# Eight batches of block 4's keys and values made around the last batch's routing, in place of two behind it

## The chip, the cores and the metric

The kernel runs on one core of a Trainium2 chip. The metric is the time of one execution on the device, in microseconds (us). A core has five engines with instruction queues of their own: TensorE (PE; its weight loads are shown as PEld), VectorE (DVE), ScalarE (ACT), GpSimd (POOL) and SyncE (SP, which only issues DMAs here). Each works its queue off in order and waits at semaphores.

## The reference

A decoder of two layers on 16 sequences ("batches" below) of 256 rows by 256 columns, in float32, with residual additions. Cut to what matters here, its six blocks are:

```python
x = x + self_attention_16_heads(layernorm(x))                       # block 0
x = x + cross_attention_16_heads(layernorm(x), ctx, mask)           # block 1
t = rmsnorm(layernorm(x)) * norm_weight                             # block 2: experts
g, e = top_k(t @ gate_w.T, 2)                                       # routing
x = x + layernorm(x) + sum(softmax(g)[k] * mlp(expert e[k], t))
x = x + linear_attention(layernorm(x))                              # block 3
x = x + cross_attention(layernorm(x), ctx @ Wk.T, ctx @ Wv.T)       # block 4
x = x + gated_expert_attention(layernorm(x))                        # block 5
```

The keys and values of block 4, `ctx @ Wk.T` and `ctx @ Wv.T`, depend on nothing but the inputs. They can be made at any time before block 4.

## The kernel before

The whole of x stays on the chip (`xs[b]`, 128 partitions by 2 by 256 for each batch). The work is staged:

- Stage 0 and 1 (pool `s01`, blocks 0 and 1): a software pipeline over `duos`, the 2 x 16 x 4 pairs of head pairs. `step(n)` (L638) issues the projections of duo n, the scores of n-1, the transposes of n-2 and the weighted sums of n-3. Behind the pipeline, a generator `route(b)` (L515) for each batch does the routing of block 2. It is resumed once per step; what lies between two of its `yield`s goes into one step. For the last batch, 15, step 131 (`len(duos) + 3`) starts it (norm of the rows, store of them to `hd`), step 133 makes the transposes `ps_hT` (L543), step 134 the logits `lgp` (L547) and from them on VectorE the two largest and the gates, step 136 the counts `pp` (L586), `cps` and the four scatters into `perms` (L608), step 137 `pb` (L620) and the last addition to x (L623). Batch 14 is four steps ahead: its `pp` and `cps` are in step 132, its `pb` in step 133.
- Stage 2 (pool `s2`, block 2): set-up from the counts, `plan()` (L818, first matmuls `ps_tok`, L821), then 71 expert tiles.
- Stage 3 (pool `s3`, block 3): `SETS`, four for each batch; `step3(s)` (L1119) issues the scores of set s (`scores3`, L1035), the weighted sums of s-2 and the finish of s-3, and at given sets of a batch the gather, sums, statistics, norm (`normed3`, L983, whose `h` is written at L988), transposes (`rows3`, L997) and projections of later batches.
- Stages 4 and 5: blocks 4 and 5.

The order of TensorE's instructions is the order in which they are written (`tc.manual_schedule`), in stage 3 that of VectorE too. The other queues are ordered by a planner, which takes the instruction that it expects to be ready.

`context4(b, ...)` (L289) is a generator that makes the keys and the values of block 4 for batch b. Its three pieces are: the load of the transposed ctx rows `c` (`ctx_rows`, L78, 256 KB on SP); the keys, 8 matmul records `ps_k`, a copy to `k4` on ScalarE (L297) and the store to `kd` from ScalarE's queue (L298); the values, `ps_v`, `v4` (L304) and `vd` (L305), likewise. `fill(gens, n, ahead)` (L308) resumes the first unfinished generator n times, and each time that one ends, it starts the load of the one that stands `ahead` places behind.

Two batches (`EARLY`) are made at the end of stage 1: their generators and weights `w4` are set up at step 127, and `fill(early, 2 * EARLY)` (L715) runs all four halves behind the last step, so behind the last batch's `pb`. Their tiles are slots of pool `s01`: `c` has two, which block 1's ctx rows use too, `k4` takes those of `qk`, and `v4` those of `v`, six of which two hold the weights. The other 14 batches are made in stage 3 (`late`): eight halves by `fill(late, 8, 2)` (L1165) ahead of the steps, three in each of the steps -3, -2 and -1, and one in each of the steps 0 to 10 (L1168).

Behind the last early half the pool `s01` is closed. The next instructions are memsets of `ve` on GpSimd (L728), loads of `ph` from `perms` on SP (L756) and a chain of small operations from `ti` (L761) to `pick` (L810), which `plan` needs; their tiles lie where those of `s01` lay.

Of the kernel before, what the change touches and what calls it, by code (L numbers as in the profile page):

```python
# [10 lines left out]
F32 = mybir.dt.float32  # L11
# [6 lines left out]
P = 128  # L18
D = 256
S = 256  # L20
NEG = -3.0e38
EARLY = 2


@with_exitstack
def decoder(ctx: ExitStack, tc: tile.TileContext, a: dict, out: bass.AP):
# [48 lines left out]

    dram = ctx.enter_context(tc.tile_pool(name="dram", bufs=1, space=bass.MemoryType.DRAM))

    def ctx_rows(b, pool, bufs=2):  # L78

        ct = pool.tile([P, 2, S], F32, tag="c", name="c", bufs=bufs)  # L80
        nc.sync.dma_start(
            out=ct, in_=a["ctxT"][:, b * S : (b + 1) * S].rearrange("(c p) s -> p c s", p=P)
        )
        return ct
# [111 lines left out]
    def two_k(ps, lhsT, rhs):  # L196

        for c in range(2):
            nc.tensor.matmul(ps, lhsT=lhsT(c), rhs=rhs(c), start=(c == 0), stop=(c == 1))  # L199
# [88 lines left out]

    def context4(b, pool, mm, wk, wv, kt, vt, cpool=None):  # L289

        ct = ctx_rows(b, cpool or pool, 3 if cpool else 2)
        yield
        ps = mm([P, 2, S], "ps_k4")
        for m in range(2):
            two_k(ps[:, m, :], lambda c: wk[:, c, m * P : (m + 1) * P], lambda c: ct[:, c, :])
        k = pool.tile([P, 2, S], F32, tag=kt[0], name="k4", bufs=kt[1])
        nc.scalar.copy(k, ps)  # L297
        nc.scalar.dma_start(out=kds[b], in_=k)  # L298
        yield
        ps = mm([P, 2, D], "ps_v4")  # L300
        for t in range(2):
            two_k(ps[:, t, :], lambda c: ct[:, c, t * P : (t + 1) * P], lambda c: wv[:, c, :])
        v = pool.tile([P, 2, D], F32, tag=vt[0], name="v4", bufs=vt[1])
        nc.scalar.copy(v, ps)  # L304
        nc.scalar.dma_start(out=vds[b], in_=v)  # L305
        yield

    def fill(gens, n, ahead=1):  # L308

        for _ in range(n):  # L310
            while gens and next(gens[0], 0) == 0:
                gens.pop(0)
                if len(gens) > ahead:
                    next(gens[ahead])
# [32 lines left out]
    with ExitStack() as st:  # L347
        pool = st.enter_context(tc.tile_pool(name="s01", bufs=2))
# [35 lines left out]
        def rows_T(l, b):  # L384
            ps = transposed(hs[l, b], psum, "mm", bufs=4)
            hTs[l, b] = hp.tile([P, 2, S], F32, tag="hT", name="hT")
            nc.scalar.copy(hTs[l, b], ps)
# [247 lines left out]
        duos = [(l, b, d) for l in range(2) for b in range(NB) for d in range(4)]  # L635
        routing = []

        def step(n):  # L638
            at = [duos[n - k] if 0 <= n - k < len(duos) else None for k in range(4)]
            new, sc, tr, av = at  # L640

            if n >= 4 and n - 4 < len(duos) and duos[n - 4][2] == 3:
                output(duos[n - 4][0], duos[n - 4][1], 1)
            if sc:
                for i in range(2):
                    scores(sc[0], sc[1], 2 * sc[2] + i)
            if av:
                for i in range(2):
                    weighted(av[0], av[1], 2 * av[2] + i)
            others = []  # L650
            if av and av[2] == 3:
                others.append(lambda: output(av[0], av[1], 0))
            if new:
                l, b, d = new
                nxt = duos[n + 4] if n + 4 < len(duos) else None
                if d < 3:
                    others.append(lambda: values(l, b, d + 1))
                if nxt and d == 1:
                    prepare(nxt[0], nxt[1])
                if nxt and d == 2:  # L660
                    others.append(lambda: rows_T(nxt[0], nxt[1]))
                if nxt and d == 3:
                    others.append(lambda: values(nxt[0], nxt[1], 0))
            turns = [[] for _ in range(4)]
            if new:
                for i in range(4):
                    turns[i].append(lambda i=i: project(l, b, 2 * d + i // 2, i % 2))

            rest = [x for t in turns for x in t] + others
            trs = []  # L670
            if tr:
                trs = [lambda i=i: heads_T(tr[0], tr[1], 2 * tr[2] + i // 2, i % 2) for i in range(4)]
            for i, x in enumerate(rest):
                x()
                if i >= 1 and trs:
                    trs.pop(0)()
            for x in trs:
                x()
            for g in list(routing):
                if next(g, 0) == 0:  # L680
                    routing.remove(g)
            if n >= 4 and n - 4 < len(duos) and duos[n - 4][0] == 1 and duos[n - 4][2] == 3:
                routing.append(route(duos[n - 4][1]))
                next(routing[-1])

        with tc.manual_schedule(engines={mybir.EngineType.PE}):
            prepare(0, 0)
            rows_T(0, 0)
            values(0, 0, 0)
            n = 0  # L690
            early = []
            while n < len(duos) + 4 or routing:
                if n == 2:
                    wts[1] = load_attention("x0")
                    for p in perms:
                        nc.sync.dma_start(out=p.rearrange("(p f) o -> p (f o)", p=P), in_=zero)
                if n == 4 * NB + 4:
                    load_moe()
                if n == len(duos) - 1:
                    w4 = []  # L700
                    for name, cols in (("x1_wqk", slice(D, 2 * D)), ("x1_wv", slice(0, D))):
                        w = pool.tile([P, 2, D], F32, tag="v", name="w4", bufs=6)
                        nc.sync.dma_start(
                            out=w, in_=a[name][:, cols].rearrange("(c p) e -> p c e", p=P)
                        )
                        w4.append(w)
                    early = [
                        context4(b, pool, mm_tile, *w4, ("qk", 2), ("v", 6))
                        for b in range(EARLY)
                    ]  # L710
                    next(early[0])
                    next(early[1])
                step(n)
                n += 1
            fill(early, 2 * EARLY)  # L715

# [13 lines left out]
    with ExitStack() as st:  # L732
        pool = st.enter_context(tc.tile_pool(name="s2", bufs=2))
# [19 lines left out]
        for i in range(4):  # L753
            for hf in range(2):
                n = P * P
# [196 lines left out]
    with ExitStack() as st:  # L952
        pool = st.enter_context(tc.tile_pool(name="s3", bufs=2))
# [155 lines left out]
        def added3(b):  # L1109
# [3 lines left out]

        late = [
            context4(b, pool, mm3, wxqk[:, :, D : 2 * D], wxv, ("k4", 1), ("v4", 1), vep)
            for b in range(EARLY, NB)
        ]
# [107 lines left out]
    with ExitStack() as st:  # L1225
        pool = st.enter_context(tc.tile_pool(name="s4", bufs=2))
# [170 lines left out]
    with ExitStack() as st:  # L1397
        pool = st.enter_context(tc.tile_pool(name="s5", bufs=2))
# [161 lines left out]
```

## Time and profile before

| What | Value |
|---|---|
| median of 3 runs | 3849.63 us (3846.42 to 3852.25) |
| the profiled execution's own time | 3849.59 us |
| its span, first to last instruction | 3847.9 us |
| granted TensorE clock over the span | 0.99 |
| TensorE, VectorE, ScalarE, GpSimd busy | 97%, 59%, 42%, 27% |
| DMA | 171.44 MB, mean 45 GB/s |
| HBM read, written | 139.57 MB, 27.69 MB |

A row of a timeline gives the start in us from the span's first instruction, the duration, the engine, the line of the kernel, the operation, the tile written and the tiles read, the shapes and the number of instructions merged; in brackets stands how long the engine had been idle before and what ended the wait. A row of a table of stretches gives the stretch, its length, the busy time of PE, PEld, DVE, ACT and POOL with the number of instructions, the granted TensorE clock (1.00 is full), the share of time in which the 16 DMA engines were busy, and GB/s. TensorE's busy time holds matmuls whose ends are modelled, so a busy TensorE isn't always at its peak.

Stage 1 ends at about 1677 us, the early batches run until 1686, `plan` begins at 1697, the last expert tile ends at 1976, and stage 3 lasts from there to about 2338.

### The profile page before, as it was taken

The page shows a single profiled execution, that of the slowest core. Times are in us where ns is not written, and L with a number is a line of the kernel's source. Part 1 is how long each engine was busy: PE and PEld are TensorE (multiplying, and loading weights), DVE is VectorE, ACT ScalarE, POOL GpSimd, SP SyncE. Part 2 cuts the span into 40 slices and gives each one's busy share as a digit, 9 for nine tenths or more (in the row PEclk, how much of TensorE's full clock was granted, in tenths as well). Part 3 has the DMA queues.
Part 4 walks back from the last instruction along what each step waited for, and adds up shares of the span by engine and source line. Part 5 has one row for each costly group of instructions (what it writes and reads, how often), then busy time and mean ns, then how long its engine had stood idle before and what let it go on. Part 6 is the DMA issues. An engine that isn't in the chain of part 4 may idle for free.

```text
span 3847.9 us, 64735 instructions
## 1 busy us (share of the span) xinstructions
PE 3716.0 (97%) x23638; PEld 2715.6 (71%) x23638; DVE 2276.2 (59%) x6213; ACT 1618.1 (42%) x4871; POOL 1041.1 (27%) x1467
## 2 busy tenths in 40 slices
PE   8999999999999999979999889999999999999999
PEld 6777776777777777759987666665666666666666
DVE  6666667645555555532226786776655555555554
ACT  4555554555555555524445555665221222122111
POOL 3332332233343343332225553222000000000100
PEclk9999999999999999979999999999999999999999
DMA  5000000010000000032234000001222222222222
GB/s 196 1 1 1 1 1 1 1 58 15 12 17 18 9 18 17 18 91 72 71 120 151 28 19 25 29 29 24 69 60 59 62 68 61 61 59 66 62 62 50
DMA packets 88268, 171.44 MB, mean 45 GB/s; under 512 B 12448, under 2 KB 60584, under 8 KB 79760
## 3 DMA queue, kind: packets, MB, share of 16 engines
q1 hardware_dynamic: 74384, 141.16, 13.5%
q0 software_dynamic: 8528, 17.74, 1.7%
q10 hardware_dynamic: 5040, 8.40, 0.6%
q8 instruction: 189, 3.10, 0.3%
q14 instruction: 127, 1.04, 0.1%
HBM read 139.57 MB, written 27.69 MB: 43 GB/s over the span
## 4 chain that ended last, share of the span: by engine, by line
PE 87%; DVE 11%; issue 1%; ACT 1%; POOL 0%; DMA 0%; DVEq 0%; POOLq 0%; ACTq 0%
PE ps_qk L199 14%; PE po L1468 11%; PE ps_ve L199 11%; PE ps_v L199 7%; PE tr L268 6%; PE po L505 6%; PE sc L237 4%; PE ps_h L199 3%; PE po L892 3%; PE av L274 3%; PE sc L433 2%; PE av L490 2%; PE sc L1315 2%; PE sc L1289 2%; PE zt L1328 1%; DVE sc L443 1%
## 5 line engine op out<-in xcount | busy, mean ns | idle before, releaser
L258 POOL TENSOR_TENSOR pr<-pr,sm 128x256 f32<-128x256 f32 (+1 forms) x384 | 310.2, 829 | 1449.0 <-DVE sm L256 1337.5
L252 ACT ACTIVATE pr<-sc,nmx 128x128 f32<-128x128 f32 (+1 forms) x768 | 315.3, 417 | 350.8 <-DVE nmx L250 313.6
L1468 PE MATMUL po<-w_oe,ut 128*128 128x256 f32 x2048 | 452.4, 379 | 0.0
L199 PE MATMUL ps_ve<-w_ve,hT 128*128 128x512 f32 x1024 | 450.9, 593 | 0.0
L1468 PEld LDWEIGHTS po<-w_oe,ut 128*128 128x128 f32 x2048 | 388.8, 190 | 52.9 <-issue 0.2
L269 ACT COPY pT<-tr 128x512 f32<-128x512 f32 (+1 forms) x256 | 136.1, 532 | 649.8 <-PE tr L268 649.8
L268 PEld LDWEIGHTS tr<-ident,pr 128*128 128x128 f32 x2176 | 270.8, 141 | 167.9 <-issue 117.5
L268 PE MATMUL tr<-ident,pr 128*128 128x128 f32 x2176 | 346.7, 275 | 13.6 <-ACT zT L499 10.3
L199 PEld LDWEIGHTS ps_ve<-w_ve,hT 128*128 128x128 f32 x1024 | 191.3, 190 | 215.3 <-issue 207.1
L448 ACT ACTIVATE pr<-sc,nmx 128x256 f32<-128x256 f32 x512 | 237.1, 472 | 251.1 <-DVE nmx L443 174.2
L454 POOL TENSOR_TENSOR pr<-pr,sm 128x512 f32<-128x512 f32 x256 | 264.4, 1055 | 282.6 <-DVE sm L452 141.9
L1440 DVE TENSOR_TENSOR tv<-ps_ve,gm 128x512 f32<-128x512 f32 x256 | 176.4, 689 | 204.9 <-PE ps_ve L199 198.2
L443 DVE CUSTOM_DVE_ANT_0 sc<-sc,mk 128x256 f32<-128x256 f32 x512 | 211.0, 443 | 112.0 <-PE sc L433 59.4
L250 DVE TENSOR_REDUCE nmx<-sc 128x2 f32<-128x256 f32 (+1 forms) x384 | 208.1, 556 | 110.1 <-ACT pr L252 105.4
L199 PE MATMUL ps_qk<-hT,w_a 128*128 128x256 f32 x1024 | 259.8, 387 | 0.0
L269 DVE COPY pT<-tr 128x384 f32<-128x384 f32 (+1 forms) x384 | 223.1, 594 | 19.1 <-PE tr L268 13.1
L199 PEld LDWEIGHTS ps_qk<-hT,w_a 128*128 128x128 f32 x1024 | 180.6, 191 | 29.4 <-issue 11.8
L199 PE MATMUL ps_qk<-hT,w 128*128 128x256 f32 x768 | 183.3, 382 | 0.7 <-DVE zn L939 0.7
L1295 DVE TENSOR_REDUCE nm<-sc 128x4 f32<-128x1024 f32 x128 | 150.7, 1220 | 33.6 <-PE sc L1289 33.6
L237 PE MATMUL sc<-qk 64*128 64x128 f32 (+1 forms) x1536 | 160.9, 341 | 4.7 <-ACT pr L252 2.1
L868 DVE COPY wt<-m_w 128x1024 f32 x71 | 49.3, 694 | 188.0 <-PE ps_h L199 186.2
L1459 DVE TENSOR_TENSOR ut<-gr,av 128x1024 f32<-128x1024 f32 x128 | 155.0, 1212 | 5.1 <-PE av L279 5.1
(277 smaller groups left out, 7020.8 us busy)
## 6 DMA issues: line engine op xcount, KB each, us to landing
gr<-gd SPq DMA_DIRECT2D x128, 512.0 KB
yd<-y SPq DMA_DIRECT2D x71, 128.0 KB
c<-in_ctxT SPq DMA_DIRECT2D x32, 256.0 KB
m_w<-in_m_w SPq DMA_DIRECT2D x16, 512.0 KB
x<-in_x SPq DMA_DIRECT2D x16, 256.0 KB
mk<-in_mask SPq DMA_DIRECT2D x16, 256.0 KB
hd<-h SPq DMA_DIRECT2D x16, 256.0 KB
kd<-k ACTq DMA_DIRECT2D x16, 256.0 KB
```

Source lines behind the costliest of these rows:

```text
L199: nc.tensor.matmul(ps, lhsT=lhsT(c), rhs=rhs(c), start=(c == 0), stop=(c == 1))
L237: nc.tensor.matmul(sc[:, j, at : at + ks], lhsT=qk[rows, 0, qs], rhs=qk[rows, 1, 0:ks], start=True, stop=True,)
L250: nc.vector.tensor_reduce(nmx[:, qt, :], sc[:, :, sl], AX.X, ALU.max, negate=True)
L252: nc.scalar.activation(pr[:, j, sl], sc[:, j, sl], AF.Exp, bias=nmx[:, qt, j : j + 1], accum_out=sm[:, qt, j : j + 1],)
L258: nc.gpsimd.tensor_tensor(pr[:, :, sl], pr[:, :, sl], sm[:, qt, :].unsqueeze(2).to_broadcast([P, 2, n]), ALU.mult,)
L268: nc.tensor.transpose(tr[:, at : at + P], src, ident)
L269: copy(pT, tr[:, 0 : P * len(blocks)])
L443: nc.vector.tensor_tensor_reduce(out=sc[:, j, t, :], in0=sc[:, j, t, :], in1=mk[:, t, :], scale=-1.0, scalar=3.4e38, op0=ALU.add, op1=ALU. ...
L448: nc.scalar.activation(pr[:, j, t, :], sc[:, j, t, :], AF.Exp, bias=nmx[:, j, t : t + 1], scale=-1.0, accum_out=sm[:, j, t : t + 1],)
L454: nc.gpsimd.tensor_tensor(pr[:, j], pr[:, j], sm[:, j, :].unsqueeze(2).to_broadcast([P, 2, S]), ALU.mult)
L505: nc.tensor.matmul(po, lhsT=zTs[l, b, c][:, t * P : (t + 1) * P], rhs=wts[l][3][:, c, :], start=(c == 0), stop=(c == 7),)
L1468: nc.tensor.matmul(po[:, t, :], lhsT=ut[:, e, t * P : (t + 1) * P], rhs=woe[hp][:, e, :], start=(hp == 0 and e == 0), stop=(hp == 3 and e ...
```

## The change

`EARLY` becomes 8. Three loads are started at step 127. Behind step 132 (batch 14's `pp` and `cps`; batch 15 is being normalised) four halves are run, behind step 135 (batch 15's logits are being sorted out) two, and behind the last step all that are left, which are ten. The ctx rows of the early batches take the slots of `c` and of `mk`, block 1's mask tile, in turn. Stage 3 has eight batches left, sixteen halves, in the same calls of `fill`.

```diff
-EARLY = 2
+EARLY = 8
...
-    def ctx_rows(b, pool, bufs=2):
+    def ctx_rows(b, pool, bufs=2, tag="c"):
-        ct = pool.tile([P, 2, S], F32, tag="c", name="c", bufs=bufs)
+        ct = pool.tile([P, 2, S], F32, tag=tag, name="c", bufs=bufs)
...
     def context4(b, pool, mm, wk, wv, kt, vt, cpool=None):
-        ct = ctx_rows(b, cpool or pool, 3 if cpool else 2)
+        if cpool:
+            ct = ctx_rows(b, cpool, 3)
+        else:
+            ct = ctx_rows(b, pool, 2, ("c", "mk")[b % 2])
...
-                    next(early[0])
-                    next(early[1])
+                    for g in early[:3]:
+                        next(g)
                 step(n)
+                if n == len(duos) + 4:
+                    fill(early, 4, 2)
+                if n == len(duos) + 7:
+                    fill(early, 2, 2)
                 n += 1
-            fill(early, 2 * EARLY)
+            fill(early, 2 * EARLY, 2)
```

## The prediction

> **What bounds the kernel now.** I read the page's busy shares first, then the table of stretches around the last batch's routing, the timeline of TensorE there, the chain that ended last across it, and the table of stretches by batch of stage 3.
>
> ```profile
> span 3847.9 us, 64735 instructions
> PE 3716.0 (97%) x23638; PEld 2715.6 (71%) x23638; DVE 2276.2 (59%) x6213; ACT 1618.1 (42%) x4871; POOL 1041.1 (27%) x1467
> ```
>
> TensorE is busy for 97% of the span, so work moved helps only where TensorE now waits, and only if nothing else ends last where it came from. The stretches (us; busy time of PE, PEld, DVE, ACT, POOL; granted clock; DMA share and GB/s) of the routing's end:
>
> ```profile
> 1655.00:1665.50 10.50, 1.68 (x10) 0.93 (x9) 5.65 (x32) 0.36 (x1) 5.12 (x5) 0.61 0.70 225
> 1665.50:1676.70 11.20, 6.75 (x22) 4.64 (x22) 4.32 (x28) 1.15 (x3) 1.05 (x2) 0.50 0.39 72
> 1676.70:1686.10 9.40, 9.40 (x33) 7.59 (x32) 0.69 (x1) 1.76 (x3) 2.81 (x3) 0.76 0.21 63
> 1686.10:1697.40 11.30, 0.02 (x1) 0.00 (x0) 5.45 (x29) 0.59 (x1) 3.71 (x24) 0.74 0.80 224
> ```
>
> TensorE is nearly idle in the first and the last of them, and its clock is down to a half in the second. The same in TensorE's timeline (start, duration, in brackets the idle time before):
>
> ```profile
> 1655.15 0.38 PE L616 MATMUL cps<-ident,cb 128*8 128x128 f32 x2
> 1656.04 1.12 PE L622 MATMUL pb<-b,cT 8*128 8x256 f32 x4 [0.51 <-ACT cT L618]
> 1665.47 1.30 PE L191 MATMUL ps_hT<-ident,h 128*128 128x128 f32 x4 [8.31 <-DVE h L535]
> 1672.16 0.61 PE L588 MATMUL pp<-both,tri 128*128 128x16 f32 x2 [2.78 <-DVE both L570]
> 1676.71 3.78 PE L199 MATMUL ps_k<-c,w 128*128 128x256 f32 x8
> 1684.23 1.89 PE L199 MATMUL ps_v<-w,c 128*128 128x256 f32 x8
> 1697.47 0.89 PE L821 MATMUL ps_tok<-pick,ph 128*128 128x71 f32 x3 [11.35 <-DVE pick L810]
> ```
>
> So the three gaps: 8.31 us (rows of batch 15 being normalised), 2.78 us (its two largest logits), 11.35 us (between the early batches and `plan`). The third is no free room. What follows the last early matmul, in time order:
>
> ```profile
> 1686.15 0.59 ACT L304 COPY v<-ps_v 128x512 f32<-128x512 f32 x1 [1.14 <-PE ps_v L199]
> 1686.77 0.33 ACTq L305 DMA_DIRECT2D vd<-v  x1
> 1689.23 1.85 POOL L728 MEMSET ve<- 128x1024 f32 x2 [9.11 <-DMA vd<-v]
> 1691.33 0.20 DVE L763 CAST tf<-ti 128x71 f32<-128x71 int32 x1 [13.82 <-POOL ti L761]
> ```
>
> GpSimd, idle for 9.11 us, starts the next stage's set-up only when the last early batch's store has landed, and `pick`, which `plan` needs, follows from that. The 11.35 us are a tail behind the last early batch, wherever that ends. And the four-set batches 0 to 5 of stage 3, from one batch's first score matmul to the next's (same columns):
>
> ```profile
> 2013.25:2032.26 19.01, 19.01 (x159) 14.91 (x158) 11.59 (x31) 12.01 (x24) 9.45 (x10) 1.00 0.53 170
> 2032.26:2053.41 21.15, 21.15 (x202) 16.45 (x201) 13.01 (x40) 12.85 (x27) 8.96 (x8) 1.00 1.07 379
> 2053.41:2075.11 21.70, 21.32 (x201) 16.36 (x200) 14.57 (x48) 12.67 (x26) 10.29 (x18) 1.00 0.42 145
> 2075.11:2093.95 18.84, 17.05 (x177) 12.06 (x176) 13.76 (x45) 9.88 (x21) 10.66 (x15) 1.00 0.10 29
> 2093.95:2113.85 19.90, 16.97 (x176) 12.16 (x176) 15.80 (x50) 10.78 (x24) 11.62 (x21) 1.00 0.10 28
> 2113.85:2135.19 21.34, 17.75 (x177) 13.01 (x177) 15.90 (x50) 10.70 (x24) 11.62 (x21) 0.92 0.09 25
> ```
>
> The first three carry 4, 4 and 3 half batches (a K or a V, 8 matmul records, 1.73 us apart where they run back to back at full clock, as from 1978.51 to 1980.24) and have TensorE full; the next three carry none and are hardly shorter: there TensorE waits 2.2 us a batch for `h` (L988) of VectorE. Nine such batches, from the score matmuls at 2093.95 to those at 2278.72, take 184.77 / 9 = 20.5 us each. What the fills cost in stage 3 is thus far less than their 1.73 us.
>
> **The change, part by part.** Six batches (12 halves) leave stage 3; four halves go into the first gap, two into the second, ten, instead of four, behind the routing.
>
> *First gap.* 4 x 1.73 = 6.9 us start at 1655.53, behind batch 14's `cps`. `pb` of batch 14 (1.12 us) is queued behind them and ends at about 1663.6, still before `h` is there (1665.47): no cost. If that cover were gone, each half is 1.73 us. On the way: per batch one 256 KB load on SP (0.41 us of issue, loaded ahead: c of batch 1 was issued at 1631.70), per half a copy of 0.59 us and a store issue of 0.33 us on ACT, which in this stretch is busy for 0.36 us of 10.5. SP's next blocking entry is the store of `h` (1665.84), and the loads behind it are needed only after 1674. TensorE is then less cold: transposes to the copy of tT took 1.39 us here, 0.69 for batch 14 at full clock (1644.42 to 1645.11): -0.70. `lgp` to the copy of lg 1.91 against 0.99 (1650.44 to 1651.43): -0.92.
>
> *Second gap.* 2 x 1.73 = 3.46 us where the wait from lg to `pp` is 2.75 us: +0.7; `pp` is queued behind them. From `pp` to the end of `pb` it took 4.62 us, for batch 14 at full clock 2.37 (1654.79 to 1657.16): -2.25. The V copy (0.59 us) stands before the copy of cT on ACT: +0.5.
>
> *Behind the routing.* Four halves took 9.44 us (1676.71 to 1686.15, half of it at the low clock); ten at 1.73 take 17.3: +7.9. The last store landed in 2.24 us by the chain that ended last; in stage 3, with loads and stores dense, v's buffer came free 2.84 (1990.33 to 1993.17) and 4.29 us (1985.42 to 1989.71) after an issue. I take 3.2: +1.0 (0 to +2). What follows up to `ps_tok` is as now.
>
> Gaps together: -0.70 - 0.92 + 0.7 - 2.25 + 0.5 + 7.9 + 1.0 = **+6.2 us** on `plan`'s start. Bounds: +4.7 without the last store's and ACT's term; +10 if the clock stays low (the three gains of 3.87 us gone).
>
> The clock rows above (0.61, 0.50) come after 8.3 us idle, and the wait that remains before the transposes is 1665.47 - 1663.6 = 1.9 us. The Trainium skill, "TensorE: Matmul & The Clock Gate", section "HAM oscillation — how this bites in real kernels", has the array fall to half rate only behind idle gaps of over about 3.4 us: by it the 3.87 us are safe and the sum is +6.2. The trace speaks half against it: behind a wait of only 2.20 us in stage 3 one batch's `po` (L1104) took 2.98 us at 2122.82, where others took 1.89; by that row the gains may fail and the sum be +10. I keep +6.2, since the work before the wait is dense.
>
> *Stage 3.* The eight halves ahead of its steps (L1165) and eight of the nine in steps -3 to -1 stay. The ninth stands directly before the first scores: -1.8. Batch 0 (four halves): in its first two sets VectorE runs at, the rstd chain with h (4.0 us), at, qk, and ACT ks behind it with no break, so that the third scores, 7.88 us after the first, come no sooner (-0.1); the other two sets lose a half each, -3.5. Batch 1: 21.15 against an unfilled batch, which has less from VectorE here (no `added3` yet); I take 20.5 less the 1.0 that L154 loses at 2097.20 (1.19 us against 0.17 at 2078.41, beside GpSimd's L1059, which comes late there because of the rsqrt that `added3` puts on GpSimd), 19.5: -1.65. Batch 2: 21.70 against 20.5: -1.2. Batch 3, now 18.84 because VectorE enters it without arrears from the filled ones, becomes a steady one: +1.7. Sum: -1.8 - 3.6 - 1.65 - 1.2 + 1.7 = **-6.6 us**. Bounds: four steady batches, 82.0, against the present 80.7, less 1.8: -0.5; all 12 halves at 1.82 (1.73 and the start of the next scores): -21.8. The steady batches are the nearest rows, being the same work without fills, hence -6.6.
>
> Total: +6.2 - 6.6 = -0.4 us. The profiled execution took 3849.59 us (span 3847.9 and 1.7 around it), the median of the runs 3849.63: **3849.2 us**. What is not priced, the same gathers, the weights' loads at step 10 and stages 4 and 5, only starts at another time.
>
> **Rivals.** *TensorE is what bounds stage 3's start*, as its full 19.01, 21.15 and 21.32 us say, and everything that is taken out is gained: +6.2 - 21.8 = -15.6, 3834 us. For it: no idle time there. Against: the unfilled 19.90 with TensorE at 16.97. In between lie shorter unfilled first batches, about -5.
>
> *The queue of VectorE turns the first gap's fill into a delay (slower).* x <- x,pb of batch 14 (L623) stands on VectorE between L154 and L155 of batch 15's rsqrt (1657.20 and 1657.81). `pb` now ends at 1663.6. If L623 keeps its place, all behind it (the rest of rsqrt, h, and batch 14's slots for GpSimd's four scatters) starts 1664.4 - 1657.8 = 6.6 us later: 3849.2 + 6.6 = 3855.8. It decides as soon as L623 stands before L535. Against: the order of VectorE is not written by hand here, and a planner that sees `pb` late puts L623 later.
>
> *The stores can't follow (slower).* Ten stores, some three loads and the three kd/vd loads of stage 4 are 16 x 262 KB = 4.2 MB in 17.3 us, 242 GB/s against 225 at most in the rows. At the pace of stage 3's start (K copy 1978.83 to V copy 1993.17, 14.34 / 7 = 2.05 us a half) ten take 20.5: +3.2, 3852.4 us.
>
> That the change doesn't do what it says holds for the third "gap": five of eight batches stand in no gap at all, which the sum contains.
>
> **How the numbers follow.** Forecast (gain and cost cancel, 3846 to 3852) 0.60; gains in full, or most of them, 0.15; VectorE's queue 0.12; stores 0.13. The range leaves out the first rival's end and a sum of both slow ones: 3840 to 3857 us. Beyond 0.2% (7.7 us, about what a measurement of this kernel can tell): faster 0.18 (the first rival, and a little of the forecast with a better stage 3), slower 0.14 (the slow rivals together or with the low clock), within 0.68.
>
> **What would show it.** In the changed profile: TensorE busy from 1655 to 1663 and waiting under 3 us for L535; granted clock near 1 up to the last early half; `ps_tok` some 6 us later, at about 1703.7, still 11 to 13 us behind the last `ps_v`; stage 3's first batches at 15.4, 19.5 and 20.5 us with waits for L988. The prediction is wrong if `ps_tok` starts with no tail behind the last half, if L535 comes later than now, or if the unfilled first three batches take under 17 us each.

## The result, and the profile after

| | before | after |
|---|---|---|
| median of 12 runs each | 3849.57 us (3846.42 to 3856.48) | 3853.31 us (3850.09 to 3860.78) |
| span of the profiled execution | 3847.9 us | 3851.5 us |
| ratio after/before, 95% interval | | 1.0009 (1.0001 to 1.0016) |

The changed kernel is some 3.5 us slower (0.4 to 6.2 by the interval), where 0.4 us less was forecast, so the forecast missed by about 4 us. The head of the page after:

```profile
span 3851.5 us, 64752 instructions
...
PE 3718.2 (97%) x23638; PEld 2714.1 (70%) x23638; DVE 2277.9 (59%) x6213; ACT 1618.3 (42%) x4871; POOL 1038.9 (27%) x1467
```

The work is the same, instruction for instruction on TensorE, and its busy time differs by 2.2 us. What changed is where it stands. TensorE's timeline around the routing of batch 15, after (start, duration, in brackets the idle time before and what ended it):

```profile
1655.30 1.89 PE L199 MATMUL ps_k<-c,w 128*128 128x256 f32 x8
...
1664.21 0.85 PE L191 MATMUL ps_hT<-ident,h 128*128 128x128 f32 x4 [0.79 <-DVE h L539]
1666.75 1.60 PE L199 MATMUL lgp<-gw,tT 128*128 128x8 f32 x8 [1.68 <-ACT tT L549]
1668.20 3.76 PE L199 MATMUL ps_k<-c,w 128*128 128x256 f32 x8
1671.75 2.96 PE L199 MATMUL ps_v<-w,c 128*128 128x256 f32 x8
1674.55 0.29 PE L592 MATMUL pp<-both,tri 128*128 128x16 f32 x2
...
1705.80 3.66 PE L830 MATMUL ps_tok<-pick,ph 128*128 128x71 f32 x16 [11.46 <-DMA c<-in_ctxT]
```

Gap 1 went as meant: its wait is down from 8.31 to 0.79 us. But `lgp` then waits 1.68 us for `tT`, and the two halves of gap 2 take 6.35 us where two at full clock take 3.46. The table of stretches (length, busy PE, PEld, DVE, ACT, POOL, granted clock, DMA share, GB/s) gives the reason for the second:

```profile
1668.20:1674.55 6.35, 6.35 (x17) 5.11 (x18) 2.79 (x19) 0.79 (x2) 0.00 (x0) 0.55 0.97 249
...
1676.80:1694.40 17.60, 17.53 (x81) 15.12 (x80) 0.79 (x2) 5.30 (x10) 3.86 (x4) 1.00 0.85 199
```

The clock is at 0.55 in gap 2 and full in the ten halves behind the routing. For the wait for `tT`, the timeline of ScalarE's queue, and the one piece of the chain that ended last which reaches across it:

```profile
1662.40 0.59 ACT L308 COPY v<-ps_v 128x512 f32<-128x512 f32 x1 [1.14 <-issue]
1665.74 0.33 ACTq L309 DMA_DIRECT2D vd<-v  x1
1666.11 0.59 ACT L549 COPY tT<-ps_hT 128x512 f32<-128x512 f32 x1 [3.12 <-DMA kd<-k]
```

```profile
1657.84 7.83 DMA kd<-k
```

The copy of the fourth half ends at 1662.99, but its store is issued only at 1665.74. ScalarE works in order, so the copy of `tT`, whose transposes ended at 1665.06, stands behind that. What ends the wait is the landing of another store, that of the first K, which took 7.83 us. The fourth store needs nothing from it. In the kernel's list of instructions, eight completion semaphores go round over all DMAs that SP and ACT issue, and the wait in front of this issue is for the semaphore that the first K's store had eight DMAs earlier. In every hold on ScalarE below, the DMA that is waited for is likewise the eighth before in that list.

Start times of the same instruction in both profiled executions (us):

| | before | after | difference |
|---|---|---|---|
| transposes of batch 15, `ps_hT` | 1665.47 | 1664.21 | -1.26 |
| copy of `tT` | 1666.86 | 1666.11 | -0.75 |
| copy of `lg` | 1669.41 | 1668.38 | -1.03 |
| `pp` | 1672.16 | 1674.55 | +2.39 |
| first half behind the routing | 1676.71 | 1676.80 | +0.09 |
| last early V copied (ACT) | 1686.15 | 1694.37 | +8.22 |
| first memset of `ve` | 1689.23 | 1697.57 | +8.34 |
| `plan`'s `ps_tok` | 1697.47 | 1705.80 | +8.33 |
| first `ps_k` of stage 3 | 1976.68 | 1983.11 | +6.43 |
| first scores of stage 3 | 2013.25 | 2020.10 | +6.85 |
| scores of its batch 4 | 2093.95 | 2096.32 | +2.37 |
| scores of its batch 5 | 2113.85 | 2117.78 | +3.93 |
| stage 4's first transposes | 2338.36 | 2341.59 | +3.23 |
| end of the span | 3847.9 | 3851.5 | +3.6 |

So 8.3 us are lost up to `plan`, 1.9 come back in stage 2, 4.5 in stage 3's first four batches, and 0.9 are lost again behind them. These batches after, in the same columns as before (batches 0, 1, 2, 3 and 5):

```profile
2020.10:2037.28 17.18, 13.50 (x128) 9.50 (x127) 10.98 (x30) 9.57 (x20) 9.05 (x10) 0.90 0.32 102
2037.28:2055.95 18.67, 16.37 (x169) 11.24 (x168) 13.04 (x42) 10.35 (x24) 9.07 (x9) 0.91 1.07 365
2055.95:2074.92 18.97, 17.02 (x177) 11.97 (x176) 14.22 (x47) 10.33 (x23) 9.14 (x13) 1.00 0.32 102
2074.92:2096.32 21.40, 18.04 (x176) 12.95 (x176) 15.89 (x50) 10.69 (x24) 11.60 (x21) 0.92 0.09 26
...
2117.78:2137.78 20.00, 16.95 (x177) 12.05 (x177) 15.80 (x50) 10.79 (x24) 11.62 (x21) 1.00 0.09 27
```

TensorE now has room in the first three, and they are 1.8, 2.5 and 2.7 us shorter for four, four and three halves less. Batch 3 is 2.6 us longer. And the start of stage 3 has a piece at the low clock that wasn't there before (TensorE, after):

```profile
2000.43 0.78 PE L1006 MATMUL ps_hT<-ident,h 128*128 128x128 f32 x4 [3.25 <-DVE h L997]
2001.05 3.08 PE L199 MATMUL ps_k<-c,w 128*128 128x256 f32 x8
2003.93 2.43 PE L199 MATMUL ps_v<-w,c 128*128 128x256 f32 x8
```

Behind a wait of 3.25 us (before: 2.78) the next K and V together take 1.7 us more than at full clock.

### The profile page after: what moved, and what is told of

Same layout as the page of the kernel before. It is cut to its first block, busy times and chain, and to the rows that moved or that the text cites. A ratio compares the mean times of both kernels' runs of the same rounds, so it can differ in the third digit from the quotient of the medians.

```text
span 3851.5 us, 64752 instructions
## 1 busy us (share of the span) xinstructions
PE 3718.2 (97%) x23638; PEld 2714.1 (70%) x23638; DVE 2277.9 (59%) x6213; ACT 1618.3 (42%) x4871; POOL 1038.9 (27%) x1467
## 4 chain that ended last, share of the span: by engine, by line
PE 86%; DVE 11%; issue 1%; ACT 1%; DMA 1%; POOL 0%; SPq 0%; DVEq 0%; ACTq 0%; POOLq 0%
PE ps_qk L199 14%; PE po L1477 11%; PE ps_ve L199 11%; PE ps_v L199 6%; PE tr L268 6%; PE po L509 6%; PE sc L237 4%; PE ps_h L199 3%; PE po L901 3%; PE av L274 3%; PE sc L437 2%; PE av L494 2%; PE sc L1324 2%; PE sc L1298 2%; PE zt L1337 1%; DVE sc L447 1%
## 5 line engine op out<-in xcount | busy, mean ns | idle before, releaser
L268 PE MATMUL tr<-ident,pr 128*128 128x128 f32 x2176 | 346.4, 275 | 13.4 <-ACT zT L503 10.2
```

The lines of the kernel that those rows point to most:

```text
L268: nc.tensor.transpose(tr[:, at : at + P], src, ident)
```

## The experiments

**The theory:** the six halves in the gaps are free as far as TensorE goes, but their stores are not. Each is issued from ScalarE's queue, whose next entry the routing needs; while 2.75 MB of stage 3's weights fill the DMA engines, an issue waits for an earlier DMA; TensorE then waits, its clock falls, and gap 2 runs cold. Behind the routing each half costs its 1.73 us. **The rivals:** the low clock comes from the filling itself and not from the wait; a half in gap 2 is dear in any case; what stands behind the routing is not what ends last; stage 3 takes back what is won.

All times are of `ps_tok` in a profiled execution unless called a ratio, which is that of the times to the kernel before, with its 95% interval. In the measurement of the first four kernels the kernel before took 3833.67 us, in the others 3849.36 to 3850.51. The difference is in stage 3 (an unfilled batch takes about 18.3 to 20.1 us in the former, 19.5 to 21.8 in the latter), and why is not known. Up to stage 3 the executions agree to about 1 us, and ratios are taken within one measurement. A part of that 1 us is there before anything was changed: batch 14's `pp` starts between 1653.58 and 1654.93. The table at the end gives `ps_tok` counted from it, too.

**e1_tt_vector.** The changed kernel, with the last batch's `tT` copied by VectorE:

```diff
-            nc.scalar.copy(tT, ps)
+            (nc.vector.tensor_copy if b == NB - 1 else nc.scalar.copy)(tT, ps)
```

> The changed kernel, with one copy moved: the last batch's tT (rows transposed, the input of its logits) is copied from PSUM by VectorE instead of ScalarE. In the changed kernel ScalarE stands still from 1662.99 to 1665.74 us with the store of batch 1's values in its queue, and tT is copied only at 1666.11, 1.9 us after the transposes began; TensorE waits 1.68 us for it, and then runs the two halves of the second gap in 6.35 us instead of 3.46. Theory (ScalarE's wait leaves TensorE without work, its clock falls, and the second gap's halves run at the low clock): the logits' matmuls come some 0.9 us sooner, the two halves take 3.5 to 4 us, and ps_tok (first matmul of plan) falls from 1705.8 to 1702 to 1703; about 3850 us, equal to the kernel before. Rival (the clock falls in the second gap whatever ScalarE does, since TensorE has little work there): the two halves still take over 6 us, ps_tok falls by 0.9 at most; about 3852.5 us.

Measured: `ps_tok` 1702.71, ratio 0.9999 (0.999 to 1.0008). `lgp` came at 1665.36, the wait for `tT` was 0.88 us, `pp` came at 1671.47. That is 7.83 us behind the transposes in place of 10.34, so 2.5 us less: 0.8 is the wait, the rest is the clock, which was low for half as long. The stretches of low clock, after and in e1 (same columns as above):

```profile
1667.09:1673.92 6.83, 6.83 (x21) 5.66 (x21) 2.79 (x19) 0.79 (x2) 0.00 (x0) 0.50 0.95 210
1666.41:1669.82 3.41, 3.41 (x9) 2.69 (x10) 2.79 (x19) 0.20 (x1) 0.00 (x0) 0.50 1.13 156
```

The two halves took 5.22 us, between the theory's 3.5 to 4 and the rival's 6, the first of them still 3.62: a shorter wait did not keep the clock up. In time, the ratio is back at that of the kernel before, but its interval overlaps that of the change.

**e2_no_gap2.** The changed kernel without the fill of gap 2; its two halves stand behind the routing, twelve in all:

```diff
-                if n == len(duos) + 7:
-                    fill(early, 2, 2)
```

> The changed kernel without the fill in the second gap: its two halves (batch 2) go behind the routing, where twelve halves then stand. Theory (the second gap hides next to nothing of them, since they run there at the low clock in 6.35 us where the wait is 2.75): pp comes 2.5 to 3.5 us sooner, the tail is 3.5 us longer, ps_tok within 1 us of 1705.8, and the time within 1.5 us of the changed kernel. Rival (the gap does hide its 2.75 us, and the low clock comes from elsewhere): ps_tok at 1708 to 1709 and 2.5 us more time.

Measured: 1710.51, ratio 1.0015 (1.0006 to 1.0024), beyond both expectations. `pp` came at 1670.94, but at the low clock, as did the first two halves behind the routing (3.78 and 2.81 us). The cold stretch has to be paid somewhere; in gap 2 it lies partly under the wait for the logits. Gap 2 is not what made the change dear.

**e3_gaps_only.** `EARLY = 3`: four halves in gap 1, two in gap 2, none behind the routing.

> The changed kernel with EARLY = 3: the same four halves in the first gap and two in the second, none behind the routing; stage 3 has thirteen batches left (26 halves: 8 ahead of its steps, 9 in steps -3 to -1, 9 in steps 0 to 8). Theory (what stands behind the routing is in series with plan, down to the four scatters of the last batch, which in the changed kernel are issued from 1677.2 to 1682.0 and must land too): the next stage's set-up begins at about 1684, ps_tok at about 1692.3, 5 us sooner than in the kernel before and 13.5 sooner than in the changed one; stage 3 as in the kernel before less 1 us; about 3844 us. Rival (the 11.4 us before plan are set by other work, and the halves lie beside it): ps_tok not below 1696; 3849 us or more.

Measured: 1699.22, ratio 0.9999 (0.999 to 1.0008): missed by 7 us. With no half behind the routing, `ps_tok` came 1.8 us later than before the change. `lgp` waited 5.26 us for `tT`: the fourth store was issued at 1668.18, 6.3 us behind its copy.

**e4_gap1_only.** `EARLY = 2` and no fill of gap 2: the four halves of before, all in gap 1.

> The changed kernel with EARLY = 2 and only the first gap's fill: both early batches (four halves) run in the first gap, nothing in the second, nothing behind the routing; stage 3 is that of the kernel before, 14 batches. Theory (the first gap hides its halves in full; a half behind the routing costs plan its whole time until the scatters' landing is reached): pp at 1671 to 1672, the scatters' issue ends at 1679 to 1680, ps_tok at 1689.5 to 1691, 7 us sooner than in the kernel before, and the whole of it stays: 3842 to 3843 us. It would also be sooner than the version with the second gap filled, by what that gap delays pp. Rival: as in the previous one, ps_tok not below 1696, 3848 us.

Measured: 1698.98, ratio 0.9999 (0.999 to 1.0008): missed by 8 us or more, for the same reason (the fourth store issued at 1670.44, `lgp` waited 6.41 us). And a new last: the memset of `ve` waited for the scatters, not for a store. So there is a second floor behind the halves, and in this pair it and the hold on ScalarE together cost more than the four halves behind the routing did.

**e5_early3_tt.** e3_gaps_only with `tT` on VectorE.

> Three early batches (four halves in gap 1, two in gap 2, none in the tail) and the last batch's tT copied by VectorE. Theory: with ScalarE no longer in the way of tT, the routing of e3_gaps_only moves forward as a whole: lgp near 1665 instead of 1669.2, pp near 1671 (the gap-2 halves still cold), the last scatter issued near 1678.5 and the memset of ve 6.7 us behind it, near 1685.5; ps_tok near 1693.5 instead of 1699.2, 4 us ahead of before's 1697.5. Time 5 to 6 us under e3_gaps_only: ratio to before 0.998 to 0.9988. Rival: the scatters land when the traffic around them allows, and not a fixed time behind their issue; then the memset of ve stays at 1690 to 1691 and the ratio at 0.9999.

Measured: 1692.45, 5.0 us ahead of before and 6.8 ahead of e3; ratio 0.9991 (0.9982 to 1.0). `pp` at 1671.14. GpSimd's timeline shows the floor:

```profile
1677.63 0.96 POOL L612 DMA_INDIRECT perm<-num,si  x1 [0.30 <-issue]
1684.22 1.85 POOL L737 MEMSET ve<- 128x1024 f32 x2 [5.64 <-DMA perm<-num,si]
```

The memset waits for the last scatter, 128 rows of 4 bytes, and comes 6.6 us behind its issue. That is now what ends last ahead of `plan`.

**e6_early4_tt.** e5 with a fourth batch, whose two halves stand behind the routing.

> As e5_early3_tt with a fourth early batch, whose two halves stand in the tail. Theory: the tail's two halves end near 1677 and their last store lands by 1681, while the last scatter lands near 1685.5, so they are hidden: ps_tok within 0.7 us of e5's, and stage 3 is shorter by 1.3 us (e1 against e4: 299.0 to 291.1 us of scores for six batches). Time 1 to 1.5 us under e5. Rival: every half behind the routing costs its 1.73 us of TensorE: ps_tok 3.5 us later than e5's, time 2 us over e5.

Measured: 1697.92, 5.5 us behind e5; ratio 0.9998 (0.9989 to 1.0007). The expectation failed, and so did the rival's 3.5. `pp` was 1.6 us later than in e5 (colder halves in gap 2), and the scatters with it. The rest is a longer landing: the last scatter was issued at 1679.19, the last store at 1679.32, and the memset of `ve` came at 1689.69. The chain that ended last names the scatter (10.05 us), the memset's own row the store; both were late: the scatter landed at 1689.24 by the chain, the store at 1689.07 by the trace's record of its completion. Why isn't known (the DMA engines were idle from 1684 on), so whether scatters that land in the usual 6.6 us would hide two halves isn't shown either.

**e7_w34_behind.** The changed kernel, with the weights of stage 3 held until batch 15's rstd is there, by a one-column write into their tile:

```diff
+        nc.vector.tensor_copy(
+            w34[:, 0:6144].rearrange("p (n c) -> p n c", c=512)[:, :, 0], rstds[2][:, NT - 12 : NT]
+        )
         wlqk = load_rows(w34, 0, "l_wqk")
```

> The changed kernel, tT on ScalarE, but the 2.75 MB of stage 3's weights are not requested before batch 15's rstd is there (a one-column VectorE copy into their tile makes them wait). Theory: the weights fill the DMA engines and keep the first early K's store from landing for 7.8 us, and the fourth store's issue waits for that on ScalarE. Behind the rstd they start near 1663.5, the first K's store lands in under 3.5 us, the fourth store is issued at once, tT is copied 0.7 us behind its transposes and ps_tok comes at 1702.5 to 1703.5 as in e1_tt_vector: ratio near 1.0. A later hold is possible: the store of gap 2's K waits for the store of h, which now shares the engines with the weights, and the copy of cT stands behind it: up to 3 us back. Rival: the stores are slow by themselves, or ScalarE is held by something else: the fourth store still 3 us late, tT 1.9 us behind its transposes, ps_tok near 1705.8, ratio near 1.0009.

Measured: 1709.40, ratio 1.002 (1.0011 to 1.0029). The first half of the theory held: the fourth store was issued at 1662.00, at once, and `lgp` waited 0.67 us. Then the hold came at the next place that had been named as possible, but dearer: the store of gap 2's K waited until 1675.08 for the store of `h`, now among the weights, the copy of `cT` stood behind it, `pb` waited 3.06 us, and the first half behind the routing ran cold (3.78 us).

**e8_early4_w34.** The same with `EARLY = 4`.

> Four early batches (four halves in gap 1, two in gap 2, two in the tail), tT on ScalarE, the weights behind batch 15's rstd. Theory: removing the cause does what going round it does, so within 1 us of e6_early4_tt, ps_tok 1693 to 1695, unless the store of gap 2's K holds cT (then up to 3 us more). Rival: with tT on ScalarE the wait of e3_gaps_only (5.3 us at lgp) is back and ps_tok stands at 1699 or later, ratio 0.9999 or more.

Measured: 1703.75, ratio 1.0013 (1.0004 to 1.0022). As in e7: `pp` at 1671.50, but `pb` waited 5.25 us for `cT`. Moving the traffic moves the hold.

**e9_gap1_tt.** e4_gap1_only with `tT` on VectorE.

> Two early batches, as before the change, but all four halves in gap 1, none in gap 2 and none behind the routing; the last batch's tT copied by VectorE. Theory: the four halves are free in gap 1 once ScalarE's held queue is gone round; what then ends last is the landing of the last scatter, not an early store. lgp near 1665, pp near 1669.5, last scatter issued near 1677, memset of ve 6 to 8 us behind it, 1683 to 1685, ps_tok 1691 to 1693 (before 1697.5; e4_gap1_only, with ScalarE held, 1699). Stage 3 is that of before, so all of it arrives: 4 to 6 us under before, ratio 0.9985 to 0.999. Rival: stage 3 takes back what comes before it (e5's ps_tok was 5.0 us ahead, its time 2.9): ratio 0.9995 to 1.

Measured: 1695.75, ratio 0.9994 (0.9985 to 1.0003), 3 us short of the theory. `lgp` came at 1665.66, but now the exponential of the gates was held, which VectorE's queue, and so `pp`, waits for (ScalarE):

```profile
1670.74 0.33 ACTq L309 DMA_DIRECT2D vd<-v  x1
1671.12 0.20 ACT L577 ACTIVATE g<-g 128x2 f32<-128x2 f32 x1 [8.43 <-DMA kd<-k]
```

**e10_split_tt.** e1 with the first half of gap 2 ahead of `lgp`, right behind the transposes:

```diff
-                if n == len(duos) + 7:
-                    fill(early, 2, 2)
+                if n in (len(duos) + 5, len(duos) + 7):
+                    fill(early, 1, 2)
```

> As e1_tt_vector (eight early batches, tT on VectorE), with gap 2's first half moved ahead of lgp, right behind the transposes, so that TensorE has work while tT is copied. Theory: the low clock of gap 2 comes from the two short waits ahead of lgp together (0.8 and 0.9 us, and thin work between them); with the second one filled the K half takes 1.73 us in place of 3.6, lgp comes 0.9 us later but is done at full clock, the V half behind it takes 1.73, pp comes at 1670 to 1670.5 in place of 1671.5 and ps_tok 1 to 1.5 us sooner than e1's 1702.7: ratio 0.9995 to 1.0. Rival: the clock falls whatever is in between, because of what happened before (gap 1's four halves, pb): the halves again take over 5 us together, pp at 1672.5 or later, ps_tok 1703.5 or later, ratio 1.0003 or more.

Measured: 1708.32, ratio 1.0017 (1.0008 to 1.0026). The clock did what the theory said (TensorE):

```profile
1663.77 1.89 PE L199 MATMUL ps_k<-c,w 128*128 128x256 f32 x8
1665.50 0.95 PE L199 MATMUL lgp<-gw,tT 128*128 128x8 f32 x8
1666.31 1.97 PE L199 MATMUL ps_v<-w,c 128*128 128x256 f32 x8
```

No wait, full clock, `pp` at 1669.30. But the store of gap 2's V then waited for a load of the weights, with `cT` behind it (ScalarE):

```profile
1674.38 0.36 ACT L622 COPY cT<-cps 8x256 f32<-8x256 f32 x1 [5.28 <-DMA w<-in_f_wq]
```

`pb` came 4.1 us late, and the next two halves ran cold.

**e11_early3_split.** e5 with the same split.

> As e5_early3_tt (three early batches, none behind the routing, tT on VectorE), with gap 2's first half ahead of lgp. Theory: pp 1 us sooner than e5's 1671.14 and at full clock, the scatters and ps_tok with it: 1691.5 against 1692.45; time within 1.5 us under e5, ratio 0.9985 to 0.999. Rival: as for e10_split_tt, pp 1 us later than e5's and ps_tok 1693.5; or the scatters' landing (5.6 to 6.7 us of wait so far) hides the difference, ps_tok within 0.5 us of e5's.

Measured: 1693.91, ratio 0.9982 (0.9973 to 0.9991): clearly faster than the kernel before, though `ps_tok` is 1.5 us later than e5's (0.4 us when both are counted from batch 14's `pp`). The exponential was held until 1671.62, and `pp` came at 1672.46 behind a wait of 2.89 us.

**e12_sp_stores.** By then ScalarE had been held ahead of three different instructions (`tT`, `cT`, the exponential), so the issues themselves were taken away from it. The changed kernel, early stores issued by SP:

```diff
-        nc.scalar.dma_start(out=kds[b], in_=k)
+        (nc.scalar if cpool else nc.sync).dma_start(out=kds[b], in_=k)
...
-        nc.scalar.dma_start(out=vds[b], in_=v)
+        (nc.scalar if cpool else nc.sync).dma_start(out=vds[b], in_=v)
```

> The changed kernel with the stores of its early keys and values issued by SyncE in place of ScalarE; nothing else. Theory: what held ScalarE was only these issues, each waiting for an earlier DMA; on SyncE they hold nothing that the routing needs. tT is copied 0.7 us behind its transposes (changed kernel: 1.9), cT right behind pp, the halves of gap 2 still run at the low clock, pp at 1671.3 to 1672.5, ten halves behind it, ps_tok 1702 to 1703.5 in place of 1705.8, ratio 0.9997 to 1.0002. Rival: SyncE, with the store of h, the weights and the next stage's loads behind the early stores in one queue, is late itself: the plan's loads or the store of h come later, ps_tok 1705 or later, ratio 1.0007 or more.

Measured: 1707.46, ratio 1.0016 (1.0007 to 1.0025). The routing went as the theory said, with no hold on ScalarE: `tT` 0.95 us behind the start of its transposes (after: 1.90), `cT` directly behind the V copy, `pp` at 1672.14, the first half behind the routing at 1674.39, 2.4 us sooner than in the changed kernel. Then the rival took over. All early stores, the loads of ctx rows and the weights stand in one queue now, and that was late by up to 7 us (ScalarE and TensorE):

```profile
1688.92 0.58 ACT L301 COPY k<-ps_k 128x512 f32<-128x512 f32 x1 [6.74 <-DMA kd<-k]
```

```profile
1690.81 3.49 PE L199 MATMUL ps_k<-c,w 128*128 128x256 f32 x8 [2.34 <-DMA c<-in_ctxT]
```

A K copy waited for a buffer, TensorE for ctx rows, and the last V was copied at 1696.06.

**e13_sp_split.** Both together, with all eight batches.

> As e12_sp_stores, with gap 2's first half ahead of lgp as in e10_split_tt. Theory: with neither a held ScalarE nor a low clock the forecast's sum for the gaps holds: pp near 1669.5, pb ended near 1671.5 to 1672, ten halves to 1689, ps_tok near 1700.5 (before 1697.5; e10 1708.3, where the copy of cT was held for 4.1 us), ratio 0.9993 to 0.9998: stage 3's gain is then larger than the cost. Rival: some other wait takes the place of these (the fifth wait in a row): pb later than 1674, ps_tok 1703 or later, ratio 1.0 or more.

Measured: 1705.64, ratio 1.0009 (1.0001 to 1.0018). `pp` at 1669.89 and `pb` begun at 1671.75, as expected; the ten halves started at 1672.80, 4.0 us sooner than in the changed kernel, but the last V was copied only 0.3 us sooner (1694.03), since the first half was cold (3.68 us) and the buffers came free late again (TensorE waited 1.53 us for a K copy).

**e14_early3_sp.** Stores on SP, the split, `EARLY = 3`, none behind the routing, `tT` on ScalarE.

> Three early batches, none behind the routing, one half of gap 2 ahead of lgp, stores on SyncE, tT on ScalarE. Theory: pp near 1669.5 (e11_early3_split 1672.5, where the exponential on ScalarE was held), the last scatter issued near 1676.3, the memset of ve 6.7 to 8.5 us behind it, ps_tok 1691 to 1693; ratio 0.998 to 0.9987. Rival: the scatters' landing grows as they come closer to the weights' traffic, so that nothing is gained on e11 (ps_tok 1693.9): ratio 0.9985 to 0.999.

Measured, as expected (TensorE):

```profile
1691.31 3.66 PE L830 MATMUL ps_tok<-pick,ph 128*128 128x71 f32 x16 [18.37 <-DVE pick L819]
```

6.2 us ahead of before; ratio 0.9986 (0.9977 to 0.9995). With e11 it is the fastest; both beat the kernel before and the changed one.

| kernel | halves in gap 1, gap 2, behind | held on ScalarE | low clock between the transposes and `pp` (us) | transposes to `pp` (us) | `ps_tok` | `ps_tok` counted from batch 14's `pp`, against before | ratio |
|---|---|---|---|---|---|---|---|
| before | 0, 0, 4 | none | all of it | 6.69 | 1697.47 | 0 | 1 |
| after | 4, 2, 10 | `tT` | 6.83 | 10.34 | 1705.80 | +8.4 | 1.0009 |
| e1 | 4, 2, 10 | not on the path | 3.41 | 7.83 | 1702.71 | +5.9 | 0.9999 |
| e7 | 4, 2, 10 | `cT` | 6.83 | 9.34 | 1709.40 | +13.0 | 1.002 |
| e10 | 4, 2, 10 | `cT` | none | 6.21 | 1708.32 | +12.1 | 1.0017 |
| e12 | 4, 2, 10 | none | 3.41 | 7.71 | 1707.46 | +9.9 | 1.0016 |
| e13 | 4, 2, 10 | none | none | 6.21 | 1705.64 | +8.8 | 1.0009 |
| e2 | 4, 0, 12 | `tT` | all but the start | 6.98 | 1710.51 | +13.4 | 1.0015 |
| e6 | 4, 2, 2 | not on the path | 6.83 | 9.51 | 1697.92 | +1.6 | 0.9998 |
| e8 | 4, 2, 2 | `cT` | 3.41 | 7.67 | 1703.75 | +6.7 | 1.0013 |
| e4 | 4, 0, 0 | `tT` | all but the start | 11.99 | 1698.98 | +1.6 | 0.9999 |
| e9 | 4, 0, 0 | the exponential | all but the start | 8.03 | 1695.75 | -1.4 | 0.9994 |
| e3 | 4, 2, 0 | `tT` | 10.24 | 13.75 | 1699.22 | +3.0 | 0.9999 |
| e5 | 4, 2, 0 | not on the path | 3.41 | 7.82 | 1692.45 | -4.1 | 0.9991 |
| e11 | 4, 2, 0 | the exponential | none | 8.09 | 1693.91 | -3.6 | 0.9982 |
| e14 | 4, 2, 0 | none | none | 6.21 | 1691.31 | -5.5 | 0.9986 |

No kernel with ten halves behind the routing comes before 1702; all with none come before 1699.3, and before 1696 where `tT` isn't held.

With two halves in gap 2, the way from the transposes to `pp` takes 6.21 us when the second wait is filled and nothing is held (e10, e13, e14), 7.7 to 7.8 us with one stretch of 3.41 us at the low clock (e1, e5, e8, e12), and 9.3 to 9.5 with one of 6.83 (e6, e7), all without a wait for `tT` of more than 0.9 us. The changed kernel's 10.34 is thus some 0.8 us of hold and, for the rest, low clock. That the hold also made the low clock last longer was not shown: e6 and e7 have the same 6.83 us without it.

## Why the prediction was wrong, step by step

- **First gap, the halves: right.** Four halves 1.73 us apart at full clock, `pb` behind them at 1662.30, no cost. Not foreseen was a gain: `pb` now comes too late to stand in the middle of batch 15's rsqrt, the planner put the addition to x behind `h` (L627 at 1664.38, L539 at 1663.59), and the transposes came 1.26 us sooner.
- **"Transposes to the copy of tT ... -0.70": wrong, +0.51.** ScalarE was counted by its busy time ("busy for 0.36 us of 10.5") and by issues of 0.33 us; that an issue can wait was not priced. It waited 2.75 us, from 1662.99 to 1665.74. e1 (VectorE copies) and e12 (SP issues) both take that wait away.
- **"`lgp` to the copy of lg ... -0.92": -0.28.** The clock was already falling (1.60 us for a step that takes 0.95 in e10).
- **"Second gap ... +0.7": +3.42.** From the copy of lg to `pp` 6.17 us in place of 2.75. The halves ran at 0.55 of the clock; with the second of the two waits before them filled it stayed at 1.00 (e10, e13, e14). The forecast named that risk and priced it at +10 for the sum; it chose full clock "since the work before the wait is dense". The waits before were 0.79 and 1.68 us, with thin work (3.42 us busy of the 5.9 ahead of gap 2).
- **"From `pp` to the end of `pb` ... -2.25", and +0.5 for the V copy: -2.30 and 0.** Right for the clock, which was up again by then; the copy of `cT` was not delayed.
- **"Behind the routing ... +7.9": right, +8.13** (17.57 us from the first of the ten halves to the last V's copy, against 9.44). **The last landing "+1.0": +0.1** (2.58 us from issue to memset, before 2.46).
- **"Gaps together +6.2": +8.3.** The step that failed is the five terms from the transposes to `pb`: forecast -2.67 (with the V copy), measured +0.51 - 0.28 + 3.42 - 2.30 + 0 = +1.35, so 4.0 too low. They put the store's wait at its issue and a low clock in gap 2 at nothing. Without both, the same way is 2.1 (e13) and 2.0 us (e14) shorter than before the change, near the forecast; without the hold alone it is 1.2 (e1) and 1.3 us (e12) shorter, or 0.5 longer where the clock was low for 6.83 us (e6). The sooner `h` gave 1.26 of that back, the landing 0.9, and the ten halves cost 0.2 more: 2.1 remain. In e1, with the hold off the path, `ps_tok` stands 5.2 us behind that of before (5.9 from batch 14's `pp`), near the forecast's 6.2, but by other terms: `h` sooner, gap 2 colder. In e12 and e13 the stores behind the routing were late instead.
- **Stage 2, not priced: -1.9.** Its second `ps_h` took 2.02 us in place of 3.76: the clock came up one tile sooner.
- **"Stage 3 ... -6.6": -3.2.** "The ninth stands directly before the first scores: -1.8" failed: from the first `ps_k` to the first scores it is +0.4. The half is gone (-1.7), but the wait ahead of the transposes grew from 2.78 to 3.25 us, and the K and V behind it ran cold, +1.7. In e10 and e13, where they didn't, the way from these transposes to the first scores is 17.98 us against 19.71 before, the 1.7 less that was forecast. Batches 0 to 3 together, forecast -4.75, measured -4.48 (-1.83, -2.48, -2.73, +2.56 against -3.6, -1.65, -1.2, +1.7): the sum was right, the parts were not. The other kernels with eight early batches in the same range of times (e7, e10, e12, e13) save 3.2 to 5.4 us there. Batch 4, taken as a steady one, was 1.56 us longer; from there to stage 4 it is +0.9, less than the 1.4 us that one long batch adds (see "Open" below).
- **The sum.** +8.3 - 1.9 + 0.4 - 4.5 + 0.9 = +3.2 at stage 4, +3.6 at the end. Both main steps were off in the same direction, the gaps by 2.1 and stage 3 by 3.4; stage 2's 1.9 hid a part of it.
- **The rivals.** TensorE as the bound of stage 3: no, eleven halves less shortened three batches by 7.0 us, and batch 3 gave 2.6 back. VectorE's queue: no, the addition stood behind `h`. The stores can't follow: not in the changed kernel, whose ten halves stand 1.73 us apart (one K copy waited 4.66 us for a buffer, TensorE did not); yes in e12 and e13, where they share a queue with the loads. The rival that came true, a queue that was counted as nearly idle and is held by a wait at an issue, was not on the list.

The Trainium skill, "TensorE: Matmul & The Clock Gate", section "HAM oscillation — how this bites in real kernels", was weighed in the prediction. The section words its rule as "no PE-idle gaps >~3.4µs"; that the clock falls only behind such gaps was the prediction's reading of it. That reading gave no safe bound here: the clock was down behind waits of 0.79 and 1.68 us (after), 0.80 and 0.88 us (e1) and 0.80 and 0.73 us (e12), and stayed full when the second one was filled (e10, e11, e13, e14).

**Open:** why an unfilled batch of stage 3 takes now 20.0, now 21.4 us (after: 4 of the 10 batches 3 to 12; e13: 8 of 10). Three of the four long ones of after have the clock at 0.92, the fourth at 1.00, so the clock alone isn't it. With it goes why 5.0 us at `ps_tok` (4.1 from batch 14's `pp`) are 2.9 us of time in e5 and 3.6 are 5.0 in e11; the intervals of these two ratios overlap. Also open is whether ten halves could be hidden if the next stage's tiles didn't lie where theirs lay; that wasn't tried.

## What to carry to other kernels

A free stretch on TensorE isn't free room if what fills it ends in a DMA issued from an engine that the critical chain needs next: an issue can wait for a DMA that has nothing to do with it, and everything behind it in that queue waits too. Price such an issue by the landing times in that stretch (7.8 us here for 256 KB beside 2.75 MB of loads), not by its 0.33 us, and give it to a queue that nobody waits for, as long as that queue keeps up: with ten halves behind the routing, SP's own loads came late (e12, e13). Work that is put behind the critical chain costs its full length there (1.73 us a half), while what it frees elsewhere comes back only as far as its engine was the bound (4.5 of 19 us in stage 3's first four batches).

## What the runs showed of the hardware

- A store of 256 KB took 2.24 us (before, `vd<-v` by the chain) and 7.83 us (after, `kd<-k`, while the DMA engines moved 192 to 256 GB/s at shares of 0.81 to 1.17 in the two stretches that it lies in).
- The last of four scatters of 128 rows of 4 bytes released the memset 6.6 to 6.7 us (e5, e11, e14) to 8.6 us (e9) behind its issue, 0.96 us of it GpSimd's own, in e5 with the DMA engines at 0.02 or less of their time from 1678 on. The Trainium skill, "SBUF — State Buffer", section "The DMA setup-cost knee (why "@ 1 MiB" ≠ asymptote)", gives a transfer a roughly fixed 2 us apart from its bytes; these took three to four times that.
- In all sixteen traces the granted clock is 1.00 or 0.50, and each stretch at 0.50 lasts a multiple of 3.41 us (in gap 2: 3.41 in e1, 6.83 in after).
- The clock fell after two short waits with thin work around them, 0.80 and 0.73 us in e12, 0.79 and 1.68 us in after. One half of work in the second wait kept it up.
- At the single wait ahead of stage 3's first transposes (after: the 3.25 us shown above), the matmuls behind it ran cold at all five waits of 3.12 us or more (after, e1, e2, e7, e12), at none of the six of 2.78 us or less (before, e3, e5, e9, e11, e14), and at two of the five in between (2.94 us in e6 and 3.07 in e8, not 3.00 in e10, 3.03 in e4 and 3.11 in e13).
